# One Exp of each unit two slots sooner, an input load moved up a queue, and a new order at two other places, in a selective-scan kernel followed by a spectral filter

## The chip, the cores and the metric

The kernel runs as one launch on one NeuronCore of a Trainium2 chip, everything in float32. The metric is the device time of one launch in microseconds (us): three runs give a median. A profile of one further execution is read beside it. The engines are called as the profile calls them: PE is the matrix engine (PEld its weight loads), DVE the vector engine, ACT the scalar engine with the function tables, POOL the general engine, and SP the queue that issues nearly all DMAs.

## The reference

Two layers, one after the other, on `x` of shape (4, 128, 128, 128), that is 4 batches of 128 channels and L = 16384 positions.

```
# layer 0, with DI = 256 channels d and 16 states s
h1  = relu(x @ mlp_w1.T + b1);  xm = h1 @ mlp_w2.T + b2
x_in, z = split(xm @ in_proj_w.T)
u   = silu(causal_conv4(x_in) + conv_b)
dt, B, C = split(u @ x_proj_w.T)
delta = softplus(dt @ dt_proj_w.T + dt_proj_b);   A = -exp(A_log)
for t in range(L):                       # the scan
    h[d,s] = h[d,s] * exp(delta[t,d] * A[d,s]) + delta[t,d] * B[t,s] * u[t,d]
    y[t,d] = sum_s h[d,s] * C[t,s]
out = ((y + u * D) * silu(z)) @ out_proj_w.T
x   = silu(group_norm(out, 4 groups) * gn_w + gn_b) + x
# layer 1, with F = 4 filters
a   = relu(agg_w @ group_norm(concat(x, x), 32 groups) + agg_b)
w   = softmax(mean(a) @ wg_w.T + wg_b)            # 4 weights per batch
X   = rfft2(x)
out = irfft2(sum_f w[f] * X * (X * filt[f])) + 0.5 * x     # (irfft2, rfft2 between them left out)
```

## The kernel before

**The first block** (`block0`, layer 0) cuts each batch into NCH = 32 chunks of T = 512 positions, 128 chunks in all. The 256 x 16 states of a chunk are laid out as 8 units of 4 places: a unit is (j, r) with j one of two halves of the channels and r one of four, and a place p is one tile of 128 partitions (4 states x 32 channels) by 512 positions. For each place there is one `da` = Exp(delta * A) on ACT (L387), one scan along the positions on DVE (L405), and one product of the state with C, on DVE (L407) for places 2 and 3 and on POOL (L412) for most of places 0 and 1. The inputs of the scans at places 1 to 3 are products `hb` = du * B that POOL makes for a whole unit (L354); those of place 0 are turned on PE from `bt` tiles (L295, then L374).

Time is counted in slots. A slot n is a pair of places, so a unit is two slots and a chunk NP = 16 slots; even slots scan places 0 and 1, odd ones places 2 and 3. Every step is a small function that is put into a list `todo[slot, phase]`, and a loop at L495 runs through the slots and, within each, through the phases in a fixed order. The order of the calls is the order on each engine, since nothing is moved afterwards; engines wait for each other by semaphores alone. In slot n - 1 the phase "exps" issues the Exps that slot n scans:

```
todo[n - 1, "exps"].append(partial(exps, n))
todo[n - 1, "turn"].append(partial(dbu_turn, n))
todo[n, "scans"].append(partial(scans, n))
```

`da` of place 0 has two buffers in SBUF; those of places 1, 2 and 3 have one PSUM bank each, so that an Exp for one of these waits until DVE has finished with the previous unit's. The copies of the scan's last state for the next chunk (L408, L498) are on ACT too, and wait for DVE.

`pre(k)` (L175) makes a chunk's inputs one chunk ahead. Its slots are relative to the chunk before: `load` of the input `xt` in slot 7, the first matmuls `h1_mm` (L190) in slot 9, `h1_act` (L195) in 10, the convolution in slots 0 and 1, its two Silus and the Silu of z in slot 2 (L230, L233), `xd_act` in 4, `bc_load` (the broadcasts of B and C) in 5, the Softplus in 6 (L266), `du_pool` in 7, and the replicated loads of delta and du (`rep_load`, L311) for j = 0 in slot 9 and for j = 1 in slot 16. All these DMAs go through SP, in the order of the calls.

`finish` and `group_norm` (L501) do the two normalisations of the batch before, in the slots of the next batch: statistics, a small matmul for the mean, one for the variance, the root on ACT (`root_act`, L540), its reciprocal on DVE (`invert`, L543), then for the second norm a bias from one more small matmul (`bias_mm`, `bias_act`). The three chunks' kinds that the text uses are: chunks without normalisation work on DVE (even and odd ones differ by one product given to DVE), and the 16 norming chunks of each of batches 1 to 3 (`norming`, L329).

**The second block** (`block1`, layer 1) starts when the first has ended. It takes units of 8 channels of one batch, cuts each into three steps, and runs a pipeline over the steps t: `over_h` (PE L791, copy on ACT L793), `conjugates` (DVE L798), `over_w`, `products` (DVE), `sums`, and the way back. The four filters of 8 channels (`load_filter`, four DMAs of 520 KB) are scaled by the batch's weights on ACT (`term`, L764) and added on POOL (`mix`, L770); `products` of a unit needs the finished sum. The last batch's normalisation runs inside this block, through the same `finish`, over the steps t.

Of the kernel before, what the change touches and what calls it, by code (L numbers as in the profile page):

```python
# [33 lines left out]
P = 128  # L34
T = 512
# [10 lines left out]
def kernel(ctx: ExitStack, tc: tile.TileContext, a: dict, out: bass.AP):  # L46
# [22 lines left out]
    def const(name, shape, src):  # L69
        t = cpool.tile(shape, F32, tag=name, name=name)  # L70
        nc.sync.dma_start(out=t, in_=src)
        return t
# [32 lines left out]
    def later_constants(s):  # L105
        s.wo = const("wo", [P, NH, C], a["out_wT"].rearrange("(j p) c -> p j c", p=P))
        s.gnw = col("gn_w")
        s.gnb = col("gn_b")
        s.g0 = const("g0", [P, P], a["c_g0"])
        s.g1 = const("g1", [P, P], a["c_g1"])  # L110
        s.gam = col("gn_gamma")
        s.bet = col("gn_beta")
        s.wagg = const("wagg", [P, 2, C], a["agg_wT"].rearrange("(j p) o -> p j o", p=P))
        s.bagg = col("agg_b")
        s.wwg = const("wwg", [P, NF], a["wg_wT"])
        s.bwg = const("bwg", [P, NF], a["wg_b"].partition_broadcast(P))
        s.resw = const("resw", [P, 1], a["residual_weight"].partition_broadcast(P))
        s.eps = cpool.tile([P, 1], F32, tag="eps", name="eps")
        nc.vector.memset(s.eps, EPS)
        s.ones = cpool.tile([P, P], F32, tag="ones", name="ones")  # L120
        nc.vector.memset(s.ones, 1.0)
# [25 lines left out]
def block0(tc, s):  # L147
# [4 lines left out]
    with ExitStack() as ctx:  # L152
# [22 lines left out]
        def pre(k):  # L175
# [64 lines left out]
                    )  # L240

            def xd_act():
                xd = d["xd"] = p2.tile([NX, T], F32, tag="xd", name=f"xd_{k}")
                nc.scalar.copy(xd, ps["xd"][0:NX, :])
                bc = d["bc"] = dbc.tile([2, NS, T], F32, tag="bc", name=f"bc_{k}")
                nc.sync.dma_start(out=bc.rearrange("q s t -> (q s) t"), in_=xd[R:NX, :])
# [59 lines left out]
            def rep_load(j):  # L306
# [4 lines left out]
                        nc.sync.dma_start(out=t[m * DG : (m + 1) * DG], in_=rows)  # L311

            return [
                (-9, "pe", load), (-7, "pe", h1_mm), (-6, "act", h1_act), (-5, "pe", xm_mm), (-4, "act", xm_act),
                (0, "pe", partial(cv_mm, 0)), (1, "pe", partial(cv_mm, 1)), (2, "act", silu_act),
                (NP - 3, "pe", z_mm), (NP - 1, "act", z_act), (NP + 2, "act", z_silu), (3, "pe", xd_mm), (4, "act", xd_act), (5, "pe", dt_mm), (5, "pe", xd_turn),
                (5, "act", bc_load), (6, "act", dt_act), (7, "act", xd_turn_act), (7, "pool", partial(du_pool, 0)),
                (7, "pool", partial(du_pool, 1)), (8, "pe", partial(du_turn, 0)), (9, "act", partial(rep_load, 0)),
                (8, "pool", partial(bt_act, 0, 0, 1)), (9, "act", partial(bt_act, 0, 1, 5)),
                (10, "act", partial(bt_act, 0, 5, 8)), (11, "pe", partial(du_turn, 1)),  # L320
# [52 lines left out]
                    src = d["bt"][:, t, j * ND + place(r, 0), :, :].rearrange("p s d -> p (s d)")  # L373
                    nc.tensor.transpose(b[:, t * P : (t + 1) * P], src, s.ident)  # L374

        def exps(n):

            k, j, r, p = pair(n)
            d = st[k]
            d["da", p] = [  # L380
                (psd if p + q else p2).tile([P, T], F32, tag=f"da{p + q}", name=f"da{p + q}_{k}_{j}_{r}")
                for q in range(2)
            ]
            for q in range(2):
                m = place(r, p + q)
                c = (j * NG + p + q) * ND + m
                nc.scalar.activation(d["da", p][q], d["delta", j][:, m, :], AF.Exp, scale=s.amat[:, c : c + 1])  # L387

        def scans(n):


            k, j, r, p = pair(n)
            d = st[k]
            hb = d["hb", j, r]
            das = d.pop(("da", p))
            dve = [q for q in range(2) if by_vector(k, j, r, p + q)]
            pool = [q for q in range(2) if q not in dve]
            last = d["last", j, r, p] = tiny.tile([P, 2], F32, tag=f"st{j}_{r}_{p}", name=f"st_{k}_{j}_{r}_{p}")
            if pool:
                h = p2.tile([P, 2, T], F32, tag="h", name=f"h_{k}_{j}_{r}_{p}", bufs=3)  # L400
            for q in range(2):
                b = hb[:, p + q, :] if p + q else d.pop("b0")
                init = 0.0 if k % NCH == 0 else st[k - 1]["last", j, r, p][:, q : q + 1]
                o = das[q] if q in dve else h[:, q, :]
                nc.vector.tensor_tensor_scan(o, das[q], b, init, ALU.mult, ALU.add)  # L405
            for q in dve:
                nc.vector.tensor_tensor(hb[:, p + q, :], das[q], d["C"][:, p + q, :], ALU.mult)  # L407
                nc.scalar.copy(last[:, q : q + 1], das[q][:, T - 1 : T])  # L408
            if pool:
                q = slice(pool[0], pool[-1] + 1)  # L410
                ps = slice(p + pool[0], p + pool[-1] + 1)
                nc.gpsimd.tensor_tensor(hb[:, ps, :], h[:, q, :], d["C"][:, ps, :], ALU.mult)  # L412
                todo[n + 1, "late"].append(partial(nc.scalar.copy, last[:, q], h[:, q, T - 1]))
# [69 lines left out]
            for at, phase, f in finish(s, io, b, NP + 7, norm, agg):  # L483
                todo[at + (b + 1) * NCH * NP, phase].append(f)
        for n in range(n_chunks * NP):
            todo[n - 1, "exps"].append(partial(exps, n))
            todo[n - 1, "turn"].append(partial(dbu_turn, n))
            todo[n, "scans"].append(partial(scans, n))
            if n % 2 == 0:
                todo[n - 2, "dbu"].append(partial(dbu, n // 2))  # L490
            else:
                todo[n + 2, "sums"].append(partial(sums, n // 2))
        slots = [n for n, _ in todo]
        with tc.manual_schedule():
            for n in range(min(slots), max(slots) + 1):  # L495
                for phase in ("turn", "sums", "pe", "exps", "late", "act", "pool", "dbu", "gate", "scans", "dve", "end"):
                    for f in todo[n, phase]:
                        f()  # L498


def group_norm(s, io, b, mat, which, stat, at, then):  # L501
# [40 lines left out]
    def invert():  # L542
# [2 lines left out]

    return [
        (at, "dve", aggregate), (at, "end", mean_mm), (at + 1, "act", spread_act), (at + 3, "pe", var_mm),
        (at + 3, "act", root_act), (at + 3, "dve", invert),
    ]


def finish(s, io, b, first, norm, agg, add="dve"):
# [96 lines left out]
        ]  # L649
    c = at[2] + 5  # L650
    todo += group_norm(s, io, b, "g1", 1, lambda: g["stat"], c, middle)
    todo += [(c + 4, "pe", bias_mm), (c + 4, "act", bias_act)]
    for i in range(NCH):
        at = agg(i)
        todo += [
# [10 lines left out]
def block1(tc, s):  # L666
# [10 lines left out]
    with ExitStack() as ctx:  # L677
        def pool(name, bufs, **kw):
            return ctx.enter_context(tc.tile_pool(name=name, bufs=bufs, **kw))

        p1 = pool("fc", 1)
        p2 = pool("f2", 2)
        psa = pool("psa", 1, space=PSUM)
        psx = pool("psx", 2, space=PSUM)
# [2 lines left out]
        pso = pool("pso", 1, space=PSUM)  # L687
        psf = pool("psf", 1, space=PSUM)

        def const(name, shape):  # L690
            t = p1.tile(shape, F32, tag=name, name=name)
            nc.sync.dma_start(out=t, in_=s.a[name])
            return t

        fh = const("c_fh", [H, 2 * WF])
        fwr = const("c_fwr", [W, 2 * WF])
        fwi = const("c_fwi", [W, 2 * WF])
        ihc = const("c_ihc", [H, H])
        ihs = const("c_ihs", [H, H])
        iw = const("c_iw", [W, W])  # L700
        sign = const("c_sign", [W, 2 * HH]).rearrange("w (o r k) -> w o r k", o=1, r=2)


        small = pool("small", 1)
# [35 lines left out]
            u[n].ft = ft  # L740
        loads = defaultdict(list)
        for k, ft in enumerate(spans):
            at = ft.first - 4
            if k >= KEEP:
                at = max(at, spans[k - KEEP].last)
            loads[max(at, 0)].append(ft)

        def load_filter(ft):
            ft.t = p2.tile([H, NF, CC, 2 * WF], F32, tag="ft", name=f"ft_{ft.first}", bufs=KEEP)
# [118 lines left out]
        with tc.manual_schedule():  # L868
            load(0)
            for t in range(3 * N + LAG + 3):  # L870
                n, i = divmod(t, 3)
                if i == 0:
                    for ft in loads[n]:
                        load_filter(ft)
                    load(n + 1)
                    if n == 0:
                        for f in range(NF):
                            term(0, f)
                            if f:
                                mix(0, f)  # L880
                over_h(t)
                evict(t - LAG - 1)
                residual(t - LAG - 2)
                conjugates(t)
                products(t - 2)
                for f in todo[t, "add"]:
                    f()
                over_w(t - 1)
                back_h(t - LAG)
                back_w(t - LAG - 1)  # L890
                if i == 0:
                    if n:
                        term(n, 3)
                        mix(n, 2)
                    copies(n - 2)
                elif i == 1:
                    term(n + 1, 0)
                    term(n + 1, 1)
                    if n:
                        mix(n, 3)  # L900
                else:
                    term(n + 1, 2)
                    sums(n - 1)
                    mix(n + 1, 1)
                for phase in ("pe", "act", "dve", "end"):
                    for f in todo[t, phase]:
                        f()
# [79 lines left out]
```

## Time and profile before

| | before |
|---|---|
| median of 3 runs | 7318.06 us (7317.51 to 7325.34) |
| the profiled execution's own time | 7313.21 us |
| its span, first to last instruction | 7311.3 us |
| first scan starts, last scan ends | 49.84 us, 6489.1 us |
| busy, share of the span: DVE, POOL, ACT, PE | 95%, 94%, 84%, 82% |

The span is what the profiler saw between the first and the last instruction; the execution's own time is 1.9 us more, and the median of the runs is 4.85 us above that. A row of the page's groups gives busy time, count and mean duration of one kind of instruction, and the idle time of the engine just before them with what ended it. A row of the waits view gives who waited for whom: total us, number of times, longest. A row of the timeline gives the start, the duration, the engine and the instruction, and in brackets the idle time before it and what ended it.

### The profile page before, as it was taken

The page shows a single profiled execution, that of the slowest core. Times are in us where ns is not written, and L with a number is a line of the kernel's source. Part 1 is how long each engine was busy: PE and PEld are TensorE (multiplying, and loading weights), DVE is VectorE, ACT ScalarE, POOL GpSimd, SP SyncE. Part 2 cuts the span into 40 slices and gives each one's busy share as a digit, 9 for nine tenths or more (in the row PEclk, how much of TensorE's full clock was granted, in tenths as well). Part 3 has the DMA queues.
Part 4 walks back from the last instruction along what each step waited for, and adds up shares of the span by engine and source line. Part 5 has one row for each costly group of instructions (what it writes and reads, how often), then busy time and mean ns, then how long its engine had stood idle before and what let it go on. Part 6 is the DMA issues. An engine that isn't in the chain of part 4 may idle for free.

```text
span 7311.3 us, 90639 instructions
## 1 busy us (share of the span) xinstructions
PE 5969.1 (82%) x25908; PEld 2667.5 (36%) x25908; DVE 6949.5 (95%) x8040; ACT 6148.7 (84%) x13583; POOL 6895.5 (94%) x3188
## 2 busy tenths in 40 slices
PE   7788877888778788887777888887877888868999
PEld 2233322233223233232222323332322333348999
DVE  7999999999999999999999999999999999978677
ACT  6888888888888888888888888888888888867876
POOL 6999999999999999999999999999999999977787
PEclk8888888888888889989888898888888888889999
DMA  6666666666777767767777766677777766758666
GB/s 140 162 157 146 160 157 150 157 157 163 191 180 180 183 159 168 170 163 180 181 177 192 169 166 169 163 167 179 177 188 177 178 167 157 174 144 250 186 165 170
DMA packets 864136, 1246.34 MB, mean 170 GB/s; under 512 B 78856, under 2 KB 318608, under 8 KB 863632
## 3 DMA queue, kind: packets, MB, share of 16 engines
q1 hardware_dynamic: 863488, 1240.28, 69.0%
q8 instruction: 204, 3.34, 0.2%
q14 instruction: 300, 2.46, 0.1%
q10 hardware_dynamic: 144, 0.26, 0.0%
HBM read 996.97 MB, written 243.27 MB: 170 GB/s over the span
## 4 chain that ended last, share of the span: by engine, by line
DMA 16%; ACT 16%; DVE 12%; PE 12%; issue 5%; POOL 2%; SPq 1%; DVEq 0%; ACTq 0%; POOLq 0%
ACT da L387 6%; DVE da L405 6%; DMA xt<-in_x 3%; DMA rdelta<-dd 3%; DVE h L405 3%; DMA dd<-delta 2%; DVE hb L407 2%; DMA rB<-bc 2%; DMA of<-ob 2%; PE pp_h L190 2%; ACT L387 1%; DMA xr<-in_x 1%; ACT bt L295 1%; PE y L426 1%; PE pa L791 1%
## 5 line engine op out<-in xcount | busy, mean ns | idle before, releaser
L354 POOL TENSOR_TENSOR hb<-rdu,rB 128x1536 f32<-128x1536 f32 (+2 forms) x1536 | 3605.1, 2364 | 33.3 <-DMA rdu<-dd 28.9
L387 ACT ACTIVATE da<-rdelta,amat 128x512 f32<-128x512 f32 x4096 | 2671.9, 694 | 48.2 <-DVE h L405 45.0
L412 POOL TENSOR_TENSOR hb<-h,rC 128x1024 f32<-128x1024 f32 (+1 forms) x1072 | 2434.8, 2273 | 156.0 <-DVE h L405 140.2
L405 DVE TENSOR_TENSOR_SCAN da<-da,st,hb 128x512 f32<-128x512 f32 x1976 | 2420.8, 1268 | 10.0 <-POOL hb L354 6.7
L426 PE MATMUL y<-hb,sel 128*32 128x512 f32 x8192 | 1331.8, 726 | 4.8 <-POOL hb L412 2.9
L405 DVE TENSOR_TENSOR_SCAN h<-da,st,b 128x512 f32<-128x512 f32 x992 | 1261.4, 1272 | 57.8 <-ACT da L387 40.2
L407 DVE TENSOR_TENSOR hb<-da,rC 128x512 f32<-128x512 f32 x2040 | 1297.1, 675 | 3.0
L405 DVE TENSOR_TENSOR_SCAN h<-da,st,hb 128x512 f32<-128x512 f32 x1000 | 1254.1, 1257 | 6.7 <-ACT da L387 6.4
L374 PE MATMUL b<-ident,bt 128*128 128x128 f32 x4096 | 766.1, 311 | 511.8 <-DVE h L405 395.8
L225 PE MATMUL pp_cv<-xm,wck 128*128 128x512 f32 x2048 | 1027.3, 647 | 24.1 <-ACT zs L219 23.2
L295 ACT ACTIVATE bt<-pt_dut,xdt 128x256 f32<-128x256 f32 x2048 | 836.8, 471 | 139.8 <-PE pt_dut L284 139.6
L374 PEld LDWEIGHTS b<-ident,bt 128*128 128x128 f32 x4096 | 557.0, 159 | 1085.7 <-DVE h L405 683.1
L408 ACT COPY st<-da 128x1 f32<-128x1 f32 x2040 | 282.2, 161 | 657.4 <-DVE hb L407 654.6
L225 PEld LDWEIGHTS pp_cv<-xm,wck 128*128 128x128 f32 x2048 | 403.5, 208 | 708.8 <-issue 473.1
L190 PE MATMUL pp_h<-xt,w 128*128 128x512 f32 x512 | 399.5, 925 | 273.0 <-DMA xt<-in_x 257.9
L770 POOL TENSOR_TENSOR wb<-wb,term 128x1040 f32<-128x1040 f32 x192 | 461.0, 2401 | 91.6 <-ACT term L764 76.1
L284 PE MATMUL pt_dut<-ident,du 128*128 128x128 f32 x1024 | 209.6, 328 | 269.6 <-ACT st L408 260.3
L258 PE MATMUL pp_dt<-xd,wdt 8*128 8x512 f32 x512 | 290.1, 649 | 80.1 <-ACT pp_o L450 79.2
L422 PE MATMUL y<-u,diag 128*128 128x512 f32 x512 | 297.2, 665 | 66.6 <-DVE zs L436 65.2
L303 POOL TENSOR_TENSOR du<-delta,u 128x512 f32<-128x512 f32 x256 | 319.3, 1269 | 25.3 <-ACT delta L266 25.3
L387 ACT ACT_TABLE_LOAD x262 | 336.1, 1283 | 4.6
L284 PEld LDWEIGHTS pt_dut<-ident,du 128*128 128x128 f32 x1024 | 128.8, 158 | 565.5 <-POOL du L303 426.8
(145 smaller groups left out, 8008.9 us busy)
## 6 DMA issues: line engine op xcount, KB each, us to landing
rdelta<-dd SPq DMA_DIRECT2D x1024, 256.0 KB, 4.7
rdu<-dd SPq DMA_DIRECT2D x1024, 256.0 KB, 7.7
rC<-bc SPq DMA_DIRECT2D x512, 256.0 KB, 7.4
rB<-bc SPq DMA_DIRECT2D x512, 192.0 KB, 4.7
dd<-delta SPq DMA_DIRECT2D x256, 256.0 KB, 7.5
dd<-du SPq DMA_DIRECT2D x256, 256.0 KB, 6.5
ft<-in_filt_w SPq DMA_DIRECT2D x104, 520.0 KB, 7.0
ob<-o SPq DMA_DIRECT2D x128, 256.0 KB, 2.1
```

The costliest lines, as they stand in the source:

```text
L190: nc.tensor.matmul(ps["h", j], s.w1[:, j * P : (j + 1) * P], d["xt"], start=True, stop=True)
L225: nc.tensor.matmul(ps["cv", j], w, d["xm"][:, t : t + T], start=t == 0, stop=t == KC - 1)
L284: nc.tensor.transpose(ps["dut"][:, 2 * t + j, :], d["du"][:, j, at : at + P], s.ident)
L295: nc.scalar.activation(d["bt"][:, 2 * h + t, :, q, :], src, AF.Copy, scale=d["xdt"][:, 2 * h + t, R + q : R + q + 1])
L354: nc.gpsimd.tensor_tensor(hb[:, p : p + n, :], d["du", j][:, m : m + n, :], d["B"][:, p - 1 : p - 1 + n, :], ALU.mult)
L374: nc.tensor.transpose(b[:, t * P : (t + 1) * P], src, s.ident)
L387: nc.scalar.activation(d["da", p][q], d["delta", j][:, m, :], AF.Exp, scale=s.amat[:, c : c + 1])
L405: nc.vector.tensor_tensor_scan(o, das[q], b, init, ALU.mult, ALU.add)
L407: nc.vector.tensor_tensor(hb[:, p + q, :], das[q], d["C"][:, p + q, :], ALU.mult)
L412: nc.gpsimd.tensor_tensor(hb[:, ps, :], h[:, q, :], d["C"][:, ps, :], ALU.mult)
L426: nc.tensor.matmul(y[m * DG : (m + 1) * DG, :], s.sel, d["hb", j, r][:, p, :], start=False, stop=r == NG - 1)
L770: nc.gpsimd.tensor_tensor(wb, wb, u[n].terms[f], ALU.add)
```

## The change

Four edits, and two that come with them.

1. The Exp of a unit's place 0 is taken out of the phase "exps" of the slot before its scan and issued two slots earlier, in a new phase "early" that lies after the slot's other ACT work and before its scans. The Exp of place 1 stays.
2. In `pre`, the input load of a chunk moves from slot 7 to slot 2 of the chunk before; for the very first chunk alone the broadcasts of B and C go two slots later. `xd` has one buffer in place of two.
3. In `group_norm`, the root moves from slot `at + 3` to `at + 5` and its reciprocal (and what follows from it) to `at + 6`; `bias_mm` and `bias_act` move from `c + 4` to `c + 7` and `c + 8`.
4. The seven constants of the second block are loaded in the first, with its other late constants. At the second block's start only one filter is loaded ahead of the first steps (the second one a unit later), and the four `term`s of the first unit come after its first `over_h`.

```
-                xd = d["xd"] = p2.tile([NX, T], F32, tag="xd", name=f"xd_{k}")
+                xd = d["xd"] = p1.tile([NX, T], F32, tag="xd", name=f"xd_{k}")
...
-                (-9, "pe", load), (-7, "pe", h1_mm), (-6, "act", h1_act), (-5, "pe", xm_mm), (-4, "act", xm_act),
+                (-14, "pe", load), (-7, "pe", h1_mm), (-6, "act", h1_act), (-5, "pe", xm_mm), (-4, "act", xm_act),
...
-                (5, "act", bc_load), (6, "act", dt_act), (7, "act", xd_turn_act), (7, "pool", partial(du_pool, 0)),
+                (5 if k else 7, "act", bc_load), (6, "act", dt_act), (7, "act", xd_turn_act), (7, "pool", partial(du_pool, 0)),
...
-        def exps(n):
+        def exps(n, qs):
...
-            for q in range(2):
+            for q in qs:
                 m = place(r, p + q)
                 c = (j * NG + p + q) * ND + m
-                nc.scalar.activation(d["da", p][q], d["delta", j][:, m, :], AF.Exp, scale=s.amat[:, c : c + 1])
+                da = (psd if p + q else p2).tile([P, T], F32, tag=f"da{p + q}", name=f"da{p + q}_{k}_{j}_{r}")
+                nc.scalar.activation(da, d["delta", j][:, m, :], AF.Exp, scale=s.amat[:, c : c + 1])
+                d["da", j, r, p + q] = da
...
-            todo[n - 1, "exps"].append(partial(exps, n))
+            if n % 2 == 0:
+                todo[n - 3, "early"].append(partial(exps, n, (0,)))
+            todo[n - 1, "exps"].append(partial(exps, n, (1,) if n % 2 == 0 else (0, 1)))
...
-                for phase in ("turn", "sums", "pe", "exps", "late", "act", "pool", "dbu", "gate", "scans", "dve", "end"):
+                for phase in ("turn", "sums", "pe", "exps", "late", "act", "pool", "dbu", "early", "gate", "scans", "dve", "end"):
...
-        (at + 3, "act", root_act), (at + 3, "dve", invert),
+        (at + 5, "act", root_act), (at + 6, "dve", invert),
...
-    todo += [(c + 4, "pe", bias_mm), (c + 4, "act", bias_act)]
+    todo += [(c + 7, "pe", bias_mm), (c + 8, "act", bias_act)]
...
-        fh = const("c_fh", [H, 2 * WF])
...
+        fh, fwr, fwi, ihc, ihs, iw = s.fh, s.fwr, s.fwi, s.ihc, s.ihs, s.iw
...
-            at = ft.first - 4
+            at = max(ft.first - 4, min(k, 1))
             if k >= KEEP:
                 at = max(at, spans[k - KEEP].last)
-            loads[max(at, 0)].append(ft)
+            loads[at].append(ft)
...
                     load(n + 1)
-                    if n == 0:
-                        for f in range(NF):
-                            term(0, f)
-                            if f:
-                                mix(0, f)
                 over_h(t)
+                if t == 0:
+                    for f in range(NF):
+                        term(0, f)
+                        if f:
+                            mix(0, f)
```

In the order of the built programs, POOL's instructions stand as before; on DVE only the eight reciprocals move and on PE only the four small bias matmuls; ACT and SP have the rest.

## The prediction

> **What bounds the kernel now.** I read the page's busy shares first. DVE is busy 95% and POOL 94%; the digits of DVE stand at 9 until the last five of 40 slices, where the second block runs and PE takes over (99). So in the first block, 88% of the span, DVE or POOL sets the pace.
>
> ```profile
> PE 5969.1 (82%) x25908; PEld 2667.5 (36%) x25908; DVE 6949.5 (95%) x8040; ACT 6148.7 (84%) x13583; POOL 6895.5 (94%) x3188
> ...
> PE   7788877888778788887777888887877888868999
> ...
> DVE  7999999999999999999999999999999999978677
> ```
>
> Which of the two: the waits of DVE alone, and of POOL alone, over the first block (50 to 6490 us). POOL waits for DVE 140.2 us in 225 places, 1.1 us a chunk; DVE waits for POOL in ten. DVE is the bound and POOL follows close behind. What DVE waits for is what a change can take away:
>
> ```profile
> DVE h L405 <- ACT da L387: 91.7, 99, 40.1
> DVE rstd L543 <- ACT rstd L540: 13.7, 6, 3.5
> DVE da L405 <- POOL hb L354: 7.9, 8, 1.4
> DVE da L405 <- ACT da L387: 3.2, 7, 0.8
> ```
>
> This view leaves out waits below 0.15 us; the groups have them. Their idle column before the scans:
>
> ```profile
> L405 DVE TENSOR_TENSOR_SCAN da<-da,st,hb 128x512 f32<-128x512 f32 x1976 | 2420.8, 1268 | 10.0 <-POOL hb L354 6.7
> L405 DVE TENSOR_TENSOR_SCAN h<-da,st,b 128x512 f32<-128x512 f32 x992 | 1261.4, 1272 | 57.8 <-ACT da L387 40.2
> L405 DVE TENSOR_TENSOR_SCAN h<-da,st,hb 128x512 f32<-128x512 f32 x1000 | 1254.1, 1257 | 6.7 <-ACT da L387 6.4
> ```
>
> With the first batch's rows (45.1 less the 40.1 of the launch's start, and 1.9) that is 57.8 + 10.0 + 6.7 + 5.0 + 1.9 = 81.4 us before scans. The second row, place 0 of a unit (it reads `b`), has most. Its place in the chunk comes from the timeline. Chunk 8, slots 1 to 4, ACT and DVE:
>
> ```profile
> 463.40 0.16 ACT L408 COPY st<-da 128x1 f32<-128x1 f32 x1 [2.13 <-DVE hb L407]
> ...
> 465.37 1.28 ACT L233 ACT_TABLE_LOAD   x1
> ...
> 466.67 1.06 ACT L233 ACTIVATE zs<-zs 128x1024 f32<-128x1024 f32 x1
> ...
> 468.90 1.28 ACT L387 ACT_TABLE_LOAD   x1
> ...
> 470.19 1.30 ACT L387 ACTIVATE da<-rdelta,amat 128x512 f32<-128x512 f32 x2
> ...
> 470.95 1.28 DVE L405 TENSOR_TENSOR_SCAN h<-da,st,b 128x512 f32<-128x512 f32 x1 [0.49 <-ACT da L387]
> ```
>
> ACT does the Silus of slot 2 between two table loads; the pair of Exps of slot 3 comes out late, and DVE waits 0.49 us for the first of them. After the Softplus of slot 6 it is the same at slot 8, 0.14 us. I went through the chunks: 0.49 + 0.14 stands in all 80 that don't norm, 0.14 alone in the 48 that do. And ACT had idled 2.13 us in slot 1 just before.
>
> The rest lies at slots 12 and 13 of some twenty chunks. Chunk 6:
>
> ```profile
> 381.21 0.66 SPq L185 DMA_DIRECT2D xt<-in_x  x1
> ...
> 389.51 3.78 PE L190 MATMUL pp_h<-xt,w 128*128 128x512 f32 x4 [1.92 <-DMA xt<-in_x]
> ...
> 393.33 0.69 ACT L195 ACTIVATE h<-pp_h,mlp_b 128x512 f32<-128x512 f32 x1 [0.97 <-PE pp_h L190]
> ...
> 397.25 0.47 ACT L295 ACTIVATE bt<-pt_dut,xdt 128x256 f32<-128x256 f32 x1 [1.94 <-PE pt_dut L284]
> ...
> 398.59 1.29 DVE L405 TENSOR_TENSOR_SCAN da<-da,st,hb 128x512 f32<-128x512 f32 x1 [1.05 <-POOL hb L354]
> ```
>
> `xt` lands 8 us after its issue, PE stands, ACT stands behind PE, and the Exp of slot 13 is late. The row names POOL, but POOL ended that `hb` at 393.2 (its pair began at 389.58 and took 3.57), 5.4 us earlier; the Exp ended at 398.5. In all chunks with such a wait but three (those with a root) `xt` landed later than its usual time. So this, 20 us over all chunks, is the load's doing.
>
> **The change part by part.**
>
> **Early Exp.** As many Exps and table loads as before: the new phase falls in odd slots, the Silus and the Softplus in even ones, so none of the 262 loads before an Exp (1.283 us each) is added. In slot 1 the early Exp (0.69) goes into the 2.13 us that ACT idled; it waits for its buffer, whose scan ended in the slot before. At 470.19 the Exp of place 1 then takes the spot of place 0's: ready at about 470.9, wanted at 470.46 + 1.19 = 471.65. Next in line: place 2 of slot 5, ready at 472.4 in both orders (two Exps stand ahead of it either way), wanted at 473.32, and at 472.83 when DVE is 0.49 earlier. No wait is left: -0.63 us in each of 80 chunks, -0.14 in 48: -57.
>
> Behind the early Exp on ACT stand the copies of the state and the next Exps, so it must not wait for its delta. For j = 0 the loads are issued from 487.57 on in chunk 8, median 4.7 us to landing; the early Exp is reached 3.9 us or more after the last has landed, over all chunks whose landing the trace has; for j = 1, 14 us. POOL's own dues: its products lie 1.6 us or more ahead of the scans that read them in the chunks that I followed, and its idle time (1.5 us in an even chunk, 0.9 in an odd, 0.45 in a norming one) exceeds in each pair what DVE gains.
>
> **Earlier `xt`.** Same DMA, moved on SP past `bc`, the eight broadcasts and the two stores of delta, to just behind the loads for j = 1. SP stands there waiting for ACT's `xd` (1403.2 us over 127 chunks), so nothing is delayed; the buffer has been free since slot 9 of the chunk before. PE's waits (257.9 us) go, and with them the 20 us at slots 12 and 13. Above I counted 57 + 20 = 77 of 81.4; chunk 0's first 1.7 us stays in doubt, so **-78** for both edits, 70 to 81. `xd` with one buffer is free a chunk ahead: 0.
>
> **Root.** DVE no longer meets the reciprocal before the root is done: -13.7 in the first block. But the Sqrt with its two table loads now lies ahead of slot 14's Exps. By the trace a load delays ACT by 1.3 us (469 above: load at 468.90, Exp at 470.19), so 2.6 + 0.26; place 1 of slot 14 is ready 3.35 us early in chunk 8, which covers the first norm; in the second the root comes a slot later, and place 2 of slot 15 would be some 0.8 us late, in three batches: +2.4. The Trainium skill, "ScalarE: Activation LUTs", section "What ACT_TABLE_LOAD costs", speaks against this edit: a switch costs the load and 1380 ns of drain, 2.66 us. Then two switches take 5.6 us, past the slack by 2.2 us in three places and by 3.5 in three: +17, and the edit would lose 3. The rows show no drain in the timeline; I take **-11** (+3 to -14).
>
> **Second block.** The chain before:
>
> ```profile
> 6498.93 0.38 SPq L757 DMA_DIRECT2D xt<-x  x1
> ...
> 6503.16 1.64 PE L791 MATMUL pa<-c_fh,xt 128*128 128x130 f32 x6 [9.77 <-DMA xt<-x]
> ...
> 6510.84 1.16 ACT L764 ACTIVATE term<-ft,wts 128x1040 f32<-128x1040 f32 x1 [1.23 <-DMA ft<-in_filt_w]
> 6511.90 0.46 ACT L793 COPY sa<-pa 128x384 f32<-128x384 f32 x1
> ```
>
> Without the seven constants (3.3 us of issue) `xt` goes out at about 6496.2, the landing of the last store being its new wait: 2.7 us sooner, and the filter with it. The copy at 6511.90 waited for four filters that it doesn't need; now it, `conjugates` and the next `over_h` run while the filters land, and the last term ends at about 6509.3 instead of 6512.0. What came after it in the old order (copy, 3.3 us wait, second copy, 2.1 us wait, squares at 6518.5) then starts at about 6510.6: **-8**. The block's other waits (root 5.0, DVE's 174.1 for `sa`) mostly hide behind PE: -1.5 for the root. The constants cost 3.3 us on SP in chunk 0, with 10 us to spare there. Range -4 to -12.
>
> **Start.** Scans begin when delta and du are in; DMA is saturated from 26 to 54 us (share 1.0). 256 KB of `xt` leave that stretch (1.2 us), stores of delta go first: the first scan about 2 us earlier, but POOL's first product only 1: **-1** (0 to -2).
>
> **Sum:** -78 - 11 - 9.5 - 1 = -99.5 on 7313.2, the profiled execution's time: 7213.7. The median of the runs is 4.85 above it: 7219.
>
> **The rivals.**
>
> *A new wait takes part of it.* With DVE 0.63 us sooner, place 2 of slots 5 and 9 has 0.4 to 0.6 us left, and POOL idles under 0.3 us in norming chunks. If those bring back 0.2 us a chunk (26), the roots give nothing (11) and the second block falls into PE's pace again (9.5), 53 is left: 7265. For it: PE is at 99% late in the second block. Against: every chunk repeats to 0.05 us, so there is no jitter to fall into.
>
> *The stalls are someone else's.* The waits at slots 12 and 13 could stem from PE's order rather than from `xt`: then they stay, 7239.
>
> *Slower: ACT stands at the early Exp.* It is first in line in slot 13 for the next chunk's delta; if that has not landed, ACT holds the state copies and the Exps of slot 15, which are ready 1.5 us early. From a landing 3.9 to 5.6 us later than now it costs, and each us past 1.5 more costs 127. To cross to slower by over 0.2% (14.6 us) it must eat 114 us, 0.9 a chunk: a landing some 8 us later (12 to 13 us where 4.7 is the median and 9.8 the worst of 1024). `xt` leaves that burst, which speaks against it: about 7340.
>
> *The change moves nothing,* because the Exp still waits for its buffer: excluded by the two buffers of place 0 in the order above; some weight for what I overlook: 7315.
>
> **How the numbers follow.** Main case 0.70 (own range 7206 to 7233); part lost, 0.21 with the second rival in it (7233 to 7270); nothing 0.04; slower 0.05. 0.2% is 14.6 us, about what a measurement of this kernel can tell from no change. Best end: 81.4 + 14 + 12 + 2 is 109, and 5 for the root in the second block 114: 7204. To hold 8 in 10 the range goes from there to 7252. Faster 0.92, same 0.03, slower 0.05.
>
> **What would show it.** Right: idle before `h<-da,st,b` under 5 us in place of 57.8; no wait of PE for `xt<-in_x`; the reciprocal without a wait; chunk pitches 0.63 and 0.14 us shorter; first `sa` copy of the second block before the terms. Wrong: a new row "DVE da L405 <- ACT da" or "ACT da L387 <- DMA rdelta" above 20 us, or waits for POOL's `hb` L354 in most chunks.

## The result, and the profile after

The kernel after takes 7223.5 us, median of 4 runs (7221.2 to 7228.2), where before took 7321.7 in the same comparison (7317.5 to 7328.2): a ratio of 0.9867, interval 0.9853 to 0.9882. The forecast was 7219. The profiled execution went from a span of 7311.3 us to one of 7219.4, 91.9 less: the last scan ends at 6399.9 instead of 6489.1 us (-89.2), and the second block takes 819.6 instead of 822.2 us (-2.6). That is less than the 98 of the medians because the profiled execution of before was 8.5 us shorter than this comparison's median, that of after only 2.3.

The page's shares of the span, and its digits for PE and DVE in 40 slices:

```profile
PE 5935.8 (82%) x25908; PEld 2629.2 (36%) x25908; DVE 6925.4 (96%) x8040; ACT 6133.6 (85%) x13583; POOL 6890.8 (95%) x3188
...
PE   7888888888878788888788788887787888868999
...
DVE  7999999999999999999999999999999999978677
```

Nothing changed its place: DVE paces the first block with POOL close behind, PE the last five slices. DVE's waits in the first block (us in total, times, longest), with the idle columns of the three large scan groups below:

```profile
DVE da L411 <- ACT da L392: 17.5, 17, 2.0
DVE da L411 <- issue: 4.5, 13, 0.5
DVE h L411 <- POOL hb L362: 4.0, 2, 3.7
...
DVE da L411 <- POOL hb L362: 2.0, 2, 1.1
```

```profile
L411 DVE TENSOR_TENSOR_SCAN da<-da,st,hb 128x512 f32<-128x512 f32 x1976 | 2417.4, 1265 | 22.1 <-ACT da L392 15.6 <-issue 4.5 <-POOL hb L362 2.0
L411 DVE TENSOR_TENSOR_SCAN h<-da,st,b 128x512 f32<-128x512 f32 x992 | 1256.2, 1266 | 1.5 <-PE b L382 1.5
L411 DVE TENSOR_TENSOR_SCAN h<-da,st,hb 128x512 f32<-128x512 f32 x1000 | 1249.9, 1254 | 1.4 <-ACT da L392 1.0 <-POOL hb L362 0.3
```

The second row, place 0 (`b`), went from 57.8 us of idle time to 1.5, and the reciprocal waits no more. But the first of the three went up, from 10.0 to 22.1: places 2 and 3 now wait. Chunk 8 again, slots 1 to 4, ACT and DVE:

```profile
449.81 0.72 ACT L392 ACTIVATE da<-rdelta,amat 128x512 f32<-128x512 f32 x1
452.03 0.16 ACT L414 COPY st<-da 128x1 f32<-128x1 f32 x1 [1.51 <-DVE hb L413]
...
457.53 1.28 ACT L392 ACT_TABLE_LOAD   x1
458.83 0.69 ACT L392 ACTIVATE da<-rdelta,amat 128x512 f32<-128x512 f32 x1
...
459.01 1.27 DVE L411 TENSOR_TENSOR_SCAN h<-da,st,b 128x512 f32<-128x512 f32 x1
460.20 1.25 DVE L411 TENSOR_TENSOR_SCAN h<-da,st,hb 128x512 f32<-128x512 f32 x1
```

The Exp at 449.81 is the early one, made where ACT idled before; after the Silus and the table load behind them (457.53) only the Exp of place 1 is left to do, and the scan at 459.01 waits for nothing. The pitch of such a chunk, from its first scan to the next chunk's, is 48.37 us (49.11 for an odd one) where it was 49.19 (49.94), and 50.29 instead of 50.53 for a norming one.

### The profile page after: what moved, and what is told of

Its sections match the earlier page's. It is cut to its first block, busy times and chain, and to the rows that moved or that the text cites. A ratio compares the mean times of both kernels' runs of the same rounds, so it can differ in the third digit from the quotient of the medians.

```text
span 7219.4 us, 89408 instructions
## 1 busy us (share of the span) xinstructions
PE 5935.8 (82%) x25908; PEld 2629.2 (36%) x25908; DVE 6925.4 (96%) x8040; ACT 6133.6 (85%) x13583; POOL 6890.8 (95%) x3188
## 5 line engine op out<-in xcount | busy, mean ns | idle before, releaser
L392 ACT ACTIVATE da<-rdelta,amat 128x512 f32<-128x512 f32 x4096 | 2786.1, 698 | 139.3 <-DVE h L411 134.5
L411 DVE TENSOR_TENSOR_SCAN da<-da,st,hb 128x512 f32<-128x512 f32 x1976 | 2417.4, 1265 | 22.1 <-ACT da L392 15.6
L233 PE MATMUL pp_cv<-xm,wck 128*128 128x512 f32 x2048 | 1061.0, 665 | 1.4 <-ACT xm L216 0.8
L382 PEld LDWEIGHTS b<-ident,bt 128*128 128x128 f32 x4096 | 525.5, 154 | 1242.1 <-DVE h L411 902.5
L292 PE MATMUL pt_dut<-ident,du 128*128 128x128 f32 x1024 | 233.7, 339 | 299.9 <-ACT xdt L285 174.0
L432 PEld LDWEIGHTS y<-hb,sel 128*32 128x32 f32 x8192 | 173.3, 116 | 371.4 <-issue 278.0
```

Source lines behind the costliest of these rows:

```text
L233: nc.tensor.matmul(ps["cv", j], w, d["xm"][:, t : t + T], start=t == 0, stop=t == KC - 1)
L292: nc.tensor.transpose(ps["dut"][:, 2 * t + j, :], d["du"][:, j, at : at + P], s.ident)
L392: nc.scalar.activation(da, d["delta", j][:, m, :], AF.Exp, scale=s.amat[:, c : c + 1])
L432: nc.tensor.matmul(y[m * DG : (m + 1) * DG, :], s.sel, d["hb", j, r][:, p, :], start=False, stop=r == NG - 1)
```

## The experiments

All times are medians, with the ratio to before as run beside them and its 95% interval. Pitches and idle times are those of one profiled execution, which can lie up to 21 us off its kernel's median. Of each edit only the lines that matter are shown.

**Each part alone.** Four kernels, each the kernel before with one part of the change's diff.

*The early Exp alone:*

```
-            todo[n - 1, "exps"].append(partial(exps, n))
+            if n % 2 == 0:
+                todo[n - 3, "early"].append(partial(exps, n, (0,)))
+            todo[n - 1, "exps"].append(partial(exps, n, (1,) if n % 2 == 0 else (0, 1)))
...
```

> The kernel before with the early Exp alone. Theory of the sum (only idle time goes): 0.63 us in each of 80 chunks and 0.14 in each of 48, 57 us, so about 7261. Theory of lost overlap (the profile after shows 0.82 us gained in a chunk whose idle time fell by 0.64: back-to-back scans start 1.18 us apart and last 1.27, and a wait loses that 0.09 as well as its own length): 0.82 x 80 + 0.24 x 48 = 77 us, so about 7241, with chunk pitches of 48.37 and 49.11 us where 49.19 and 49.94 were. Both: the waits behind the chunk's input at slots 12 and 13 stay (PE keeps over 200 us of waiting for xt). A rival, that the early Exp gained little and the input brought the rest: less than 40 us.

Measured: 7305.9 against 7321.4, 0.9983 (0.9977 to 0.9990). Neither sum: 16 us, a fifth of the expected 77. The profiled execution was the longest of the 21 (7326.7), so its chunks are worse than the median's. Some of them do reach 48.37 and 49.12 us, but its median chunk without a norm stands at 49.75 (even) and 50.07 (odd), above what before had. DVE's waits in the first block:

```profile
DVE da L403 <- POOL hb L354: 34.0, 26, 2.4
DVE da L403 <- ACT da L384: 28.0, 27, 1.9
DVE h L403 <- ACT da L384: 14.7, 13, 2.7
...
DVE da L403 <- issue: 13.5, 14, 2.8
```

Counted by slot, 91.6 us of idle time lie before scans of slots 12 to 14, where before has 20.3. Chunk 12 begins at 657.0 us in both kernels. First before, then the early Exp alone; PE, ACT and DVE around slot 13:

```profile
688.07 3.78 PE L190 MATMUL pp_h<-xt,w 128*128 128x512 f32 x4 [1.18 <-DMA xt<-in_x]
...
692.38 1.02 PE L422 MATMUL y<-u,diag 128*128 128x512 f32 x2
...
695.03 0.47 ACT L295 ACTIVATE bt<-pt_dut,xdt 128x256 f32<-128x256 f32 x1 [1.14 <-PE pt_dut L284]
...
695.58 1.30 ACT L387 ACTIVATE da<-rdelta,amat 128x512 f32<-128x512 f32 x2
...
696.78 2.44 DVE L405 TENSOR_TENSOR_SCAN da<-da,st,hb 128x512 f32<-128x512 f32 x2
```

```profile
687.44 3.78 PE L190 MATMUL pp_h<-xt,w 128*128 128x512 f32 x4 [1.70 <-DMA xt<-in_x]
...
691.87 1.87 PE L420 MATMUL y<-u,diag 128*128 128x512 f32 x2
...
695.36 0.47 ACT L295 ACTIVATE bt<-pt_dut,xdt 128x256 f32<-128x256 f32 x1 [2.72 <-PE pt_dut L284]
695.73 0.71 ACT L384 ACTIVATE da<-rdelta,amat 128x512 f32<-128x512 f32 x1
...
696.52 1.30 ACT L384 ACTIVATE da<-rdelta,amat 128x512 f32<-128x512 f32 x2
...
697.30 2.47 DVE L403 TENSOR_TENSOR_SCAN da<-da,st,hb 128x512 f32<-128x512 f32 x2 [1.28 <-POOL hb L354]
```

DVE now wants this scan 0.8 us sooner (slot 12 begins 36.57 us after the chunk does, and not 37.39). The row names POOL's `hb`, as the rows in the prediction did, but the Exp that the scan needs, the first of the pair, ended at 697.2, where in before it ended at 696.3. Two things make it 0.9 us later:

- The turn of du on PE, which ACT's bt needs, came 0.33 us later, although `xt` landed 0.6 us sooner. PE had waited longer for `xt` (1.70 us for 1.18), and its clock came back later: the granted clock between 690 and 693 us is 0.50 against 0.63, in the next 3 us 0.91 against 1.00, and `y`, which stands before the turn, took 1.87 us where it took 1.02.
- The other 0.6 us are the edit itself. The Exp at 695.73 is the early one for slot 14; the new order puts it between this bt and the pair for slot 13. It doesn't fill ACT's idle time here, as it does in slot 1: it stands behind the 2.72 us that ACT waits for PE.

The scan had 0.5 us to spare in before, so 0.8 and 0.9 make some 1.2 us of waiting; the row has 1.28. The wait at slot 3 had been the cover of another one at slot 13, not yet visible.

*The input alone:*

```
-                (-9, "pe", load), ...
+                (-14, "pe", load), ...
...
```

> The kernel before with the chunk's input alone (its DMA five slots sooner, xd in one buffer, the first chunk's broadcasts two slots later). The prediction's step: 20 us of idle time at slots 12 and 13, and 1 us at the start, so about 7297. With the lost overlap of some 25 waits at 0.09 us each: 23, about 7295. The rival, that PE's order and not the load makes those waits: 7318, with the waits still there. The pitch of a plain chunk (49.19 even, 49.94 odd) must not change in any of them.

Measured: 7290.3, 0.9958 (0.9945 to 0.9972). The pitches of chunks without a norm stay at 49.19 and 49.94, and 4.4 us of idle time are left at slots 12 to 14; PE's waits for `xt` in the first block are gone. So the rival that PE's order causes these waits falls. The 31 us are more than the 20 of the step. The first block's last scan ends 21.7 us sooner than in the profile of before, as predicted, but that profile was itself a short run: 7313.2, where before has medians of 7317 to 7322 in all comparisons. That the median run of before has more stalls behind `xt` than this one would explain the difference, but was not shown.

*The root alone:*

```
-        (at + 3, "act", root_act), (at + 3, "dve", invert),
+        (at + 5, "act", root_act), (at + 6, "dve", invert),
...
```

> The kernel before with the norm's root alone (root two slots later, reciprocal three). The prediction's step: 13.7 us of waits of the reciprocal go, 2.4 come back at slot 15, so 11 less in the first block and 1.5 in the second: about 7305. What the profile after suggests: six batches with a root pay 1 to 2.4 us at slot 15 for an Exp that comes late behind the Sqrt's two table loads, 10.7 us in all, so only 3 us are left: about 7315. The price of 2.66 us a table switch from the Trainium skill: 3 us slower, 7321.

Measured: 7313.7, 0.9991 (0.9984 to 0.9997), that is 2 to 12 us less, so the last of the three expectations, slower, falls. In the trace the six chunks with a root are 1.1 to 1.6 us shorter, 7.6 in all.

*The second block alone:*

```
...
+                if t == 0:
+                    for f in range(NF):
+                        term(0, f)
...
```

> The kernel before with the second block's edit alone (constants loaded in the first block, filter after the first input, the first unit's four terms after the first over_h). The prediction's step: 8 us less, so about 7310. What the profile after suggests: 2.7 us less at the end, about 7315, because PE's order puts the norm's mean matmul, which waits for ACT behind the four terms, ahead of the second over_h. No change: 7318.

Measured: 7313.4, 0.9989 (0.9981 to 0.9997). In the trace the outputs of its units come 2.2 us sooner, counted from the last scan.

Alone the four bring 16, 31, 8 and 8 us, 62 before rounding; together they bring 98. Where the other 36 are, the next kernel shows.

**Two parts together.** The kernel before with the early Exp and the input:

> The kernel before with the early Exp and the earlier input together, root and second block as before. Apart they brought 16 and 31 us. Additive theory: 46 together, about 7275. Theory of the shared deadline: the early Exp quickens DVE by 0.6 us before slot 12 but leaves the landing of xt where it was, so that PE and ACT, which stand at xt, become late for slots 12 and 13; only the earlier load lets the gain through. Then the two bring what the whole change brought less root and second block, about 80 us: 7241, with pitches of 48.37 and 49.11 us in nearly all chunks without a norm, and under 10 us of idle time at slots 12 and 13.

Measured: 7233.4 against 7316.7, 0.9884 (0.9870 to 0.9897): 83 us where the two alone make 47, so they hold the other 36 by themselves. Chunks without a norm have 48.37 and 49.12 us in the median, and idle time at slots 12 to 14 is 14.5. The theory of the shared deadline holds: with `xt` there in advance PE doesn't wait for it, and its first matmul goes at 29.2 us of chunk 12 (30.4 with the early Exp alone). Over all chunks these matmuls take 722 ns each instead of 984. The early Exp alone, then the pair:

```profile
L190 PE MATMUL pp_h<-xt,w 128*128 128x512 f32 x512 | 428.3, 984 | 280.2 <-DMA xt<-in_x 247.6 <-ACT st L406 25.3 <-ACT da L384 7.2
...
L190 PE MATMUL pp_h<-xt,w 128*128 128x512 f32 x512 | 303.9, 722 | 7.6 <-DMA xt<-in_x 4.0 <-DVE bias L132 3.6
```

**The root within the change.** First the kernel after with `root_act` and `invert` back at `at + 3`, and the bias steps at `c + 4`:

> The kernel after with the norm's root back in its old place (root and reciprocal three slots behind the sums). The prediction's step: 11 us slower than after, about 7235, with the reciprocal waiting 13 us again. What the traces of after and of the root alone suggest: 5 to 8 us slower, about 7230. If the root's new place costs as much as it saves: 7223.

Measured: 7231.4, 0.9880 (0.9867 to 0.9894); the interval overlaps that of after, so the clock alone does not settle it. In the trace the six chunks are 0.8 to 1.4 us longer than in the kernel after, 6.2 in all, and the second block's units come out 2 to 3 us later. Why not 11? With the old root DVE waits 14.2 us for the reciprocals and 2.8 more at slot 13 of the chunks with a second norm's root; with the new one 10.7 at slots 14 and 15. Chunk 33 of the kernel after, ACT and DVE:

```profile
1700.74 0.47 ACT L303 ACTIVATE bt<-pt_dut,xdt 128x256 f32<-128x256 f32 x1 [2.14 <-PE pt_dut L292]
...
1704.29 1.28 ACT L548 ACT_TABLE_LOAD   x1
1705.59 0.26 ACT L548 ACTIVATE rstd<-pp_gv,eps 128x1 f32<-128x1 f32 x1
...
1705.92 1.28 ACT L392 ACT_TABLE_LOAD   x1
1707.21 0.69 ACT L392 ACTIVATE da<-rdelta,amat 128x512 f32<-128x512 f32 x1
...
1708.00 1.28 DVE L411 TENSOR_TENSOR_SCAN h<-da,st,hb 128x512 f32<-128x512 f32 x1 [0.41 <-ACT da L392]
1711.29 2.47 DVE L411 TENSOR_TENSOR_SCAN da<-da,st,hb 128x512 f32<-128x512 f32 x2 [2.01 <-ACT da L392]
```

The switch of tables costs what the prediction read from the rows: 1.30 us from the start of the load to the root, 1.29 to the Exp. But ACT's lead had just been spent at 1700.74, on 2.14 us of waiting for PE's turn of du. The next kernel puts the root into that idle time, in slot 11:

```
+    v, r, i = ((3, 4, 6), (2, 3, 5))[which] if io.bufs == 3 else (3, 5, 6)
-        (at + 5, "act", root_act), (at + 6, "dve", invert),
+        (at + r, "act", root_act), (at + i, "dve", invert),
```

> The kernel after with the first block's roots put into slot 11 (the first norm's one slot sooner, the second's two, with its variance matmul one slot sooner), where ACT stands 1.5 to 2.1 us for PE's turn of du. Theory that the slot-15 waits come from the Sqrt's two table loads lying where ACT has no idle time: the loads go into the pocket, the six batches with a root lose their waits of 1 to 2.4 us, 5 to 10 us less than after: about 7216. If the reciprocal waits for the root again, or the turn of du is late for another reason: 7223 or more. If a switch of tables cost 2.66 us, the pocket would not hold it and the waits would stay.

Measured: 7219.6, 0.9862 (0.9849 to 0.9876), not to be told from after by the clock. In the trace the waits at slot 15 are gone, but all six chunks now wait at slot 13: 1.2 to 1.3 us in those with a first norm's root, which still become 1.2 us shorter each, and 1.0 in those with a second norm's, which gain 0.65, 0 and 0. That is 4.2 us in all, just short of what was expected. In this trace a first chunk that is 7.7 us longer than in that of after hides it. That led to the next.

**The first chunk.** In the trace of after the first chunk has 54.94 us; in those of the kernels so far it has 59 to 64. A product of 128 x 128 on DVE takes 9.07 us there in before, and 1.14 in after, where the second takes 3.42. Before, then after:

```profile
78.50 9.07 DVE L126 TENSOR_SCALAR weff<-wagg,gn_gamma 128x128 f32<-128x128 f32 x1
```

```profile
78.50 1.14 DVE L134 TENSOR_SCALAR weff<-wagg,gn_gamma 128x128 f32<-128x128 f32 x1
79.68 3.42 DVE L135 SCALAR_TENSOR_TENSOR weff<-wagg,gn_gamma,weff 128x128 f32<-128x128 f32 x1
```

A kernel before with both products on ACT and the sum on DVE:

```
-        nc.vector.tensor_scalar_mul(weff0, s.wagg[:, 0, :], s.gam[:, 0:1])
-        nc.vector.scalar_tensor_tensor(weff0, s.wagg[:, 1, :], s.gam[:, 1:2], weff0, ALU.mult, ALU.add)
+        nc.scalar.activation(weff0, s.wagg[:, 0, :], AF.Identity, scale=s.gam[:, 0:1])
+        nc.scalar.activation(weff1, s.wagg[:, 1, :], AF.Identity, scale=s.gam[:, 1:2])
+        nc.vector.tensor_add(weff0, weff0, weff1)
```

> The kernel before with the two products of the norm's weights by gamma made on ACT, and only their sum on DVE. In the profile before, the first of them, a DVE TENSOR_SCALAR of 128x128, takes 9.07 us while POOL runs tensor_tensor without a gap; in the profile after 1.14 us. Theory that DVE stands for a port that POOL holds: about 9 us less, 7312, and the pitch of the first chunk near 50.6 instead of 59.67. If the time was something else of the launch (another instruction takes the wait): 7321.

Measured: 7316.7, 0.9999 (0.9991 to 1.0007), and the chunk has 59.41 us. No gain, and the trace shows why. POOL and DVE:

```profile
82.26 3.55 POOL L356 TENSOR_TENSOR hb<-rdu,rB 128x512 f32<-128x512 f32 x2
...
78.66 7.30 DVE L129 TENSOR_TENSOR weff<-weff,weff 128x128 f32<-128x128 f32 x1 [1.78 <-ACT weff L128]
85.89 0.14 DVE L134 TENSOR_TENSOR bias<-pp_bias,agg_b 128x1 f32<-128x1 f32 x1
```

The sum of two SBUF tiles ended when POOL's row of back-to-back products did (82.26 + 3.55 = 85.81). The Trainium skill, "SBUF — State Buffer", section "Who interferes with whom", has it: a DVE instruction with two SBUF inputs takes its second through an interface that it shares with GpSimd, and contends with an instruction there that reads SBUF; with one at most, outside the two-port modes, it doesn't. How long it waits differs: here to the end of a row of POOL's instructions, in after each of the two products only to the end of one (POOL's at 79.56 and 82.95), though POOL worked without a pause there too. What decides that was not looked into. The next kernel is the one with roots in slot 11, with the second product made into PSUM:

```
+        weff1 = psum("weff1")[:, 0:C]
```

> The kernel after with the roots in slot 11, and the two products of the weights by gamma made on ACT, one of them into PSUM, so that the DVE sum has an operand in PSUM. Before, the sum of two tiles in SBUF waited 7.30 us on DVE, to the end of POOL's run of products, as the TENSOR_SCALAR had waited 9.07. Theory that a DVE instruction with all its operands in SBUF stands until POOL pauses, and one with an operand in PSUM doesn't (the scans and the products by rC, which run beside POOL all the time, each read da in PSUM): the sum takes under 1 us, and the pitch of the first chunk goes from 62.6 us in the kernel with the roots in slot 11 to 52 or 53; about 7209 in all. If any first use of these weights waits for something of the launch: 7219 again.

Measured: 7213.6, 0.9858 (0.9841 to 0.9874). DVE in the first chunk:

```profile
80.69 0.29 DVE L137 TENSOR_TENSOR weff<-weff,pp_weff 128x128 f32<-128x128 f32 x1 [3.04 <-ACT pp_weff L136]
```

0.29 instead of 7.30 us, in the middle of one of POOL's products, but 3.04 of waiting for ACT: 53.82 us for the chunk, 8.8 less than in the kernel with roots in slot 11. The three kernels that follow keep this edit, and have 0.29 us and 53.8 to 54.9 again.

**The second block's terms.** The same, with the terms at `t == 1`, behind the second `over_h`:

> The same, with the first unit's four terms of the second block put behind the second over_h instead of the first. Theory that what the prediction's step for the second block lacked is the norm's mean matmul, which waits on PE for ACT behind the four terms and holds the second over_h: with the terms one step later ACT makes the means first, PE goes on while the filter lands, and the outputs of the units (settled at 4.4 us less than before in the kernel with the roots in slot 11) come another 2 to 3 us sooner. If the filter's landing sets the start of products anyway: no change against the kernel beside it, within 1 us at the tenth copy of the block.

Measured: 7212.1, 0.9854 (0.9840 to 0.9869). PE and ACT of the kernel after at the block's start, then of this one (its last scan ends 4.5 us sooner):

```profile
6419.18 1.16 ACT L761 ACTIVATE term<-ft,wts 128x1040 f32<-128x1040 f32 x1 [0.62 <-DMA ft<-in_filt_w]
...
6420.81 0.59 PE L534 MATMUL pf_gm<-mv,g 128*128 128x1 f32 x2 [6.88 <-ACT mv L531]
...
6421.27 1.65 PE L788 MATMUL pa<-c_fh,xt 128*128 128x130 f32 x6
```

```profile
6410.45 0.59 PE L536 MATMUL pf_gm<-mv,g 128*128 128x1 f32 x2 [1.97 <-ACT mv L533]
...
6410.90 1.65 PE L791 MATMUL pa<-c_fh,xt 128*128 128x130 f32 x6
```

The second `over_h` now runs right behind the mean's matmul, 6 us earlier as counted from the last scan, because ACT makes the means before the terms. The first units come out 7.3 us sooner than before, where the kernel without this edit has 5.4; but 0.9 of the 1.9 us are there at the first `over_h` already, and the next two kernels, which keep the edit, have 5.7 and 5.8. The medians of the two differ by 1.5 us, less than either's spread. So the order of the steps is as expected, and its worth is about 1 us and not shown by the clock.

At the 51st of the 64 units the run of before gains 1.6 to 3.3 us on every other kernel, those with the old order too, so the lengths of the block say less than its first units; the cause was not looked into.

**The aggregate.** In after DVE waits 6.7 us at slot 1, all in chunks with an aggregate, where ACT's Relu waits for PE with two Exps behind it. The last kernel with this Relu one slot later (`return c + 9, c + 15, c + 16, turn_bank`):

> The kernel with roots in slot 11, the product in PUSM and the terms behind the second over_h, and further with ACT's Relu of the aggregate one slot later (behind the Exps of the next chunk's slot 1). In the profile after, DVE waits 0.5 to 1.0 us at slot 1 of chunks with an aggregate, where ACT stands up to 2.1 us at pt_agg for PE with two Exps behind it. Theory that this is the cause: the waits of slot 1 (5.6 us over the first block in the kernel without this edit) go, and with them 5 to 6 us of the first block's 6395.4; about 7206. If they are somebody else's (the early Exp, POOL): the waits stay, 7212.

Measured: 7213.7, 0.9859 (0.9843 to 0.9876): no gain. The waits of slot 1 are gone, but a new row stands first among DVE's:

```profile
DVE lg L639 <- PE pp_lg L634: 8.1, 2, 4.1
```

The end of the chain (sum, logits, softmax) counts its slots from that Relu, and came a slot later too. The kernel that follows counts from the old slot and reads the logits one slot after their matmul:

```
-    c = at[2] + 1
+    c, e = at[1] + 1, add == "dve"
-    ... (c + 4, "dve", logits_dve), (c + 5, "act", softmax_act), ...
+    ... (c + 4 + e, "dve", logits_dve), (c + 5 + e, "act", softmax_act), ...
```

> The kernel before this one with the Relu of the aggregate a slot later, but with the sum behind the last of them left in its slot, and DVE's reading of the logits one slot behind their matmul. In the kernel before this one the waits at slot 1 went (5.6 us to none), but the chain behind the last aggregate came a slot later, and DVE waited 4.1 us in each of two chunks for the logits' matmul. Theory that these 8.1 us are all that kept the gain: first block 6387 where 6395 was, about 7205 in all. If the matmul of the logits is late for PE's own sake, DVE waits in the next slot as well: 7212.

Measured: 7205.0 against 7318.6, 0.9847 (0.9833 to 0.9860), the lowest ratio of all; its interval still touches that of after. Its trace, of the shortest of its five runs, has the last scan at 6383.3 us, 16.6 sooner than after, and the second block at 813.4. The row of the logits is down to:

```profile
DVE lg L639 <- PE pp_lg L634: 2.1, 1, 2.1
```

## Why the prediction was right, and where it was not

The direction, the size and the main case held, and so did most of the signs it named: the idle time of the `b` row, no wait for `xt`, the reciprocal free, the first copy of the second block ahead of the terms. The pitches fell by more than it named (0.82 and 0.24 us for 0.63 and 0.14). The row named against it, DVE's `da` behind ACT's, stands at 17.5 us, just under the 20 given. The terms of the sum held less well than the sum: that it came within 2 us of the 98 measured is in part luck, since one term was too small and two too large.

*Early Exp and `xt`, -78.* The pair brought 83. But the step put 57 on the Exp and 20 on the load, as if each could be had alone; alone they brought 16 and 31. "No wait is left" was checked for places 2 and 3 of slot 5 and not for slots 12 and 13, where 0.5 us were to spare in chunk 12. The step asked whether the early Exp would wait for its delta, and not what ACT waits for ahead of it. And "every chunk repeats to 0.05 us" is not so in before: chunks 6, 11 and 28 are 0.8 to 1.2 us longer than their like.

Two errors inside it cancel. Idle time before scans fell less than the 77 that was taken: with the pair alone from 81.4 to 25.2 us, by 56, since other waits came up at slot 13 and, in chunks with an aggregate, at slot 1. On the other side a wait costs more than its length. Two scans in a row start 1.19 us apart and last 1.27 and 1.25; one that waits loses this overlap too. So 0.63 us of idle time gave 0.82 of pitch in a plain chunk, and 0.14 gave 0.24: 0.19 x 80 + 0.10 x 48 = 20 us that the step didn't have. Together 76, which is what the chunks from the second on gained in the trace (75.9); the medians have 83, and the trace of before is of a short run, that of the pair of its longest.

*Root, -11.* The traces show 6 to 8 in the first block. The price of a switch was right: 1.3 us by the rows, where the 2.66 of the Trainium skill's "ScalarE: Activation LUTs", section "What ACT_TABLE_LOAD costs", would have made the edit a loss of 3; the root alone gains, clear of noise. What failed is the slack: 3.35 us was read in chunk 8, which has no root, and the 2.4 us of new waits were 10.7 in the whole change. The first norm's chunks, taken as covered, have 7.1 of them.

*Second block, -9.5.* The five kernels with the new order and the terms behind the first `over_h` take 817.9 us on the mean (816.2 to 820.3), the six with the old order 822.4 (820.3 to 824.2): 4.5 less. The copy did come first, but "the next `over_h`" did not run while the filters landed: the mean's matmul stood before it on PE, and waited for ACT behind the terms (6.88 us above).

*Start, -1.* Not to be resolved: the first scan starts anywhere from 45.2 to 53.3 us in these runs. The 4.7 us that the first chunk is shorter in the trace of after are those of the two DVE products beside POOL. That is luck: the change has no part in it, since before and seven kernels with parts of the change, or all of it and other roots, have 59 us or more.

*Rivals.* "A new wait takes part of it" is what happened to the early Exp alone, at another place than named; with the pair it took some 20 us, and the overlap gave them back. "Someone else's stalls" fell with the input alone. In after ACT waited for delta only at the launch (7.1 us).

## What to carry to other kernels

A wait that is taken away moves every later deadline of its engine forward; go through the whole period and list what has less slack than the gain, because two edits can then be worth much more together (83) than apart (47), and one alone may look nearly useless. Read a slack in the very iteration that will use it, and count what stands in order behind a waiting step on each engine: work that is moved up gains nothing if it lands behind a wait. Where a step moves, look at what counts its own place from it.

## What the runs showed of the hardware that was not expected

- A DVE wait cost 0.08 to 0.10 us beyond its length, by the overlap of two instructions in a row (1.19 us from start to start, 1.27 long).
- A 128x128 product or sum on DVE took 7.30 to 10.37 us in nine traces, where it ended with a row of POOL's instructions; in after two took 1.14 and 3.42, each ending with one of them; with one operand in PSUM it took 0.29, in four traces. A BATCH_NORM_STATS2 from a single SBUF tile of 128x512 took 0.68 us on the mean.
- In chunk 12 a longer wait of PE came back twice: 0.5 us more of it, and two matmuls that followed took 0.85 us longer, at a granted clock of 0.50 against 0.63.
